# A gated delta-rule layer on one core: the older step's po and pu directly behind the newer step's px, fewer transfers, a reordered substitution

## The chip, the core and the metric

The kernel runs on one of the eight cores of a Trainium2 chip. A core has five engines with a queue of instructions each, worked through in order: TensorE (PE; its weight loads are shown apart as PEld), VectorE (DVE), ScalarE (ACT), GpSimd (POOL) and SyncE (SP), which here issues every DMA. Engines wait for one another through semaphores. [...] The metric is the device time of one execution in microseconds; less is better. Everything is float32.

## The reference

Input x is 4 sequences of 1024 rows of 256. Two residual blocks follow each other: x + layernorm(attention(layernorm(x))), and the same with a small gated feed-forward network. The attention is a gated delta rule in chunks of 64 rows, with 16 key heads, 32 value heads and 128 numbers in each head. Cut to what matters:

```python
mixed = silu(causal_conv4(x @ W_qkv.T));  q, k, v = split(mixed)      # q, k are normalized
A  = -((k * beta) @ k.T * decay) * strictly_lower
Tm = inverse(I - A)                                                    # 64 x 64, unit lower triangular
u, kcd = Tm @ (v * beta), Tm @ (k * beta * exp(gc))
def step(S, chunk):                                                    # 16 chunks, in order
    attn  = (q @ k.T) * decay
    v_new = u - kcd @ S
    out   = (q * exp(g)) @ S + attn @ v_new
    S     = S * exp(g_last) + (k * exp(g_last - g)).T @ v_new
```

The outputs are normalized by their mean square, multiplied by silu of a second projection z of x, and projected to 256 columns. The feed-forward network looks its weights up in a table of 16 numbers.

## The kernel before, in words

**Tiling.** Four value heads with their two key heads make a group; there are eight groups. A tile is a chunk of 64 rows of two sequences (halves `ab` of 128 partitions); the four sequences are two pairs, and steps alternate between the pairs, each with its own state S. A `Super` is eight steps (four chunks of both pairs) of one group, so there are 32 supers and 256 steps. The time goes into one loop of 277 slots, in which five stages of different supers lie on top of each other, so that every slot holds work for every engine.

**The generators.** Each kind of work is a Python generator that is resumed piece by piece:
- `channel` (L407): one projection of 128 columns into `pp`, the convolution on ACT (`cv`, L454) and three DVE instructions (L457), and silu (L461). Slot letter B for q and k, A for v.
- `norms` (n), `scores` (s): norms of q and k; `kkq`, the products of the chunk with itself, times the decay `dc`, into `lT` and `aT`, which go to DRAM as `ltd` and `atd`.
- `invert` (v1, v2): reads blocks of 16 from `ltd` as `lb` (L610) and inverts them by 15 pairs of DVE instructions (`rank`, `v`; L627, L629), one pair to each v1 but for the first, which calls the load. The loads of `xh` (L620) stand in its second part.
- `join` (c): puts two 16-blocks together to one of 32. ACT copies `vh_s` go to DRAM (`vth`, `vh`) and come back as the zero-padded operands `padh1` and `padh2`; products `mh1` (L662) and `mh2` (L678); the result `ndh` goes through DRAM back into `v`.
- `build` (b): the same from 32 to 64 with `pad1`, `pad2`, `mt`, `m1` (L731) and `m2` (L745). The inverse lies in DRAM as `ued`.
- `expand` (L760): loads a step's inverse `ue`, its scores `ae` (two DMAs), and `qku` (q and k).
- `step`: N0 transposes v (`pv`, L786); N1 multiplies the state (`pkqs`, L799), DVE makes `x0` (L810), ACT `qs`; N2 makes `px` (L819 transposes of k, L823 with the inverse), ACT takes `xs` and `kt` from it. In the slot after it the same generator goes on as the older one: O3 makes `po` (L848), DVE adds `core` (L862); J squares `core` on ACT; O4 makes `pu` (L875), and DVE updates S in eight instructions (L891).
- `project_out`: Z is `pz` (L145, called from L923) and its silu, POOL multiplies twice (L927, L929); T transposes (`pto`, L933) and U projects (`pout`, L940); DVE adds into `ac` (L945), which is loaded from and stored to `acc_d` for every step (L919, L949).

**What sets the order.** `SLOTS` (L1003) is the order written out by hand, one string for each of eight slots; the instructions of PE, ACT, DVE and POOL keep the order in which they are called, apart from the pieces after a `yield` of a number, which `go` resumes that many places later. SP's DMAs are placed by the framework's own scheduler. PSUM has a ring of four banks (`bank`) and one of two double banks (`two_banks`, for pp and pu): a product waits until the reader of the fourth (second) one before it is done. After the loop comes the feed-forward network, whose first part runs in the last 16 slots.

Of the kernel before, what the change touches and what calls it, by code (L numbers as in the profile page):

```python
# [14 lines left out]
P = 128  # L15
# [50 lines left out]
def delta_net_ffn_kernel(  # L66
# [258 lines left out]
    with ExitStack() as main:  # L325
# [19 lines left out]
        padh1 = w1.tile([P, NQ, C], F32, tag="padh1", name="padh1")  # L345
        padh2 = w1.tile([P, NQ, P], F32, tag="padh2", name="padh2")
        mh = w1.tile([P, NQ + 1, HB], F32, tag="mh", name="mh")
        for t in (*pads, xh, padh1, padh2, mh):
            G_.memset(t, 0.0)
        ueds = [dram.tile([P, SB * HG, C], F32, name=f"ued{i}") for i in range(3)]  # L350
        for t in ueds:
            nc.sync.dma_start(t.rearrange("p w i -> p (w i)"), pads[0].rearrange("p w i -> p (w i)"))
        states = [w1.tile([P, MG, 2, 2, P], F32, tag=f"S{p}", name="S") for p in range(NPAIR)]
# [190 lines left out]
        def scores(k, blk):  # L544
# [22 lines left out]
            for n, (u0, dc) in enumerate(zip(us, dcs)):  # L567
# [15 lines left out]
                stores = []  # L583
                for name, j, dst in (("lT", 0, k.ltd), ("aT", 1, k.atd)):
# [7 lines left out]
                    stores.append((dst[:, u0 : u0 + 2, :, :], o))  # L592
                yield 2
                for to, o in stores:
                    nc.sync.dma_start(to, o)

# [7 lines left out]
        def invert(k):  # L604
# [9 lines left out]
            yield  # L614
            for s in range(2):
                us = slice(s * SB // 2, (s + 1) * SB // 2)
                for q in range(4):
                    rows = slice(s * C + q * HB, s * C + (q + 1) * HB)
                    src = k.ltd[q * BS : q * BS + HB, us, :, q % 2 * BS + HB : (q % 2 + 1) * BS]
                    nc.sync.dma_start(xh[rows, :, s * HB : (s + 1) * HB], src.rearrange("j u h i -> j (u h) i"))  # L620
            l2, v2 = halves(lb), halves(v)
            for j in range(HB - 1):
# [5 lines left out]
                to = v2[:, :, 0 : j + 1, j + 1 :]  # L628
                V.tensor_tensor(to, to, t, ALU.subtract)  # L629
                if j < HB - 2:  # L630
                    yield
            k.lb, k.v = square(lb), square(v)

        def join(k):
# [16 lines left out]
            for s in range(2):  # L651
                for z in range(4):
                    rows = slice(z * BS + s * HB, z * BS + (s + 1) * HB)
                    u = s * 4 + z
# [20 lines left out]
            for h in range(HG):  # L675
                for q in range(4):
                    g = q * HG + h
                    T_.matmul(  # L678
                        ps[q * BS : (q + 1) * BS, h * P : (h + 1) * P],
                        lhsT=mh[:, g : g + 2, :].rearrange("p g c -> p (g c)"),  # L680
                        rhs=padh2[:, g, :],
                        start=True,
                        stop=True,
                    )
            nb = sc.tile([P, 2 * NQ, HB], F32, tag="mt", name="nbh")
            A.activation(
                nb.rearrange("p (u h) i -> p h u i", h=HG),
                ps.rearrange("p (h u i) -> p h u i", h=HG, i=HB),
                AF.Copy,
                scale=-1.0,  # L690
            )
            nc.sync.dma_start(k.ndh, nb)
# [5 lines left out]
        def build(k):  # L698
# [6 lines left out]
            for q in range(4):  # L705
                hb = slice(q % 2 * BS, (q % 2 + 1) * BS)
                to = k.ued[q * BS : (q + 1) * BS, :, hb]
                nc.sync.dma_start(to.rearrange("c w i -> w c i"), k.v[q * BS : (q + 1) * BS])
# [13 lines left out]
            for ab in range(2):  # L722
                gs = slice(ab * NQ // 2, (ab + 1) * NQ // 2)
                for z in range(4):
                    q = slice(z * BS, (z + 1) * BS)
                    nc.sync.dma_start(pad2[q, gs, q], k.ued[ab * C + BS : (ab + 1) * C, z::4, BS:])
            yield
# [26 lines left out]
            for ab in range(2):  # L754
                for hb in range(2):
                    q = slice((2 * ab + hb) * BS, (2 * ab + hb + 1) * BS)
                    to = k.ued[ab * C : ab * C + BS, hb * NQ : (hb + 1) * NQ, BS:]
                    nc.sync.dma_start(to, nb[q])

        def expand(k, u):  # L760
# [12 lines left out]
        def step(k, u):  # L773
# [18 lines left out]
            if not first:  # L792
                got = []
                for j in range(2):
# [11 lines left out]
                    got.append(ps)  # L806
                qs = t4("qs")
                for h in range(HG):
# [11 lines left out]
            for n in range(2):  # L820
                for m in range(MG):
                    for ab in range(2):
# [6 lines left out]
                        )  # L829
            xs = sc.tile([P, 2, 2, P], F32, tag="xs", name="xs")  # L830
            for ab in range(2):
                A.activation(xs[:, ab], pxs[ab][:, : 2 * P].rearrange("p (h d) -> p h d", h=2), AF.Copy, scale=-1.0)
            if not last:
                kt = sc.tile([P, 2, 2, P], F32, tag="kt", name="kt")
                for ab in range(2):
                    for n in range(2):
# [27 lines left out]
            yield  # L864
            junk = sc.tile([P, P], F32, tag="junk", name="junk")
            for h in range(HG):
                A.activation(junk, core[:, h, :], AF.Square, accum_out=k.ms[:, u, h : h + 1])  # L867
            yield
            if not last:
# [17 lines left out]
                else:  # L887
                    flat = S_.rearrange("p m a h d -> p (m a h) d")
                    made = pu.rearrange("p a (n d) -> p (a n) d", d=P)
                    for i in range(2 * HG):  # L890
                        V.scalar_tensor_tensor(  # L891
                            flat[:, i, :], flat[:, i, :], el[:, ti, i : i + 1], made[:, i, :], ALU.mult, ALU.add
                        )

        def rms(k, blk):
# [16 lines left out]
        def project_out(k, u):  # L912
# [35 lines left out]
            yield 2  # L948
            nc.sync.dma_start(acc_d[ti], ac)  # L949

# [36 lines left out]
        def work(kind, n, *args):  # L987
# [15 lines left out]
        SLOTS = [  # L1003
# [8 lines left out]
        ]  # L1012
# [154 lines left out]
        with tc.manual_schedule(engines=COMPUTE):  # L1167
            for s in range(-LQ, len(units)):
# [13 lines left out]
                if nq < len(supers):  # L1182
                    gens["B"] = channel(supers[nq], iq // 4, iq % 4, 1)
                inv = work(invert, nq - 1 if iq >= 4 else nq - 1)
                made = work(build, nq - 2)
# [118 lines left out]
```

## Time and profile before

| | |
|---|---|
| median of 3 runs | 4227.92 us (4226.19 to 4230.51) |
| the profiled execution, its own time | 4217.89 us |
| its span | 4216.2 us |
| busy: PE, DVE, ACT, POOL | 3950.7, 2919.3, 2806.3, 1930.9 us |
| first pv to last pv (the loop's steps) | 255.9 to 3889.8 us |
| DMA | 1.45 million packets, 539 MB, 52% of 16 engines |
| PE waits for DVE core before pz | 51.8 us, 32 times |
| DVE waits for lb before the first rank | 237.3 us, 32 times |

A line of the order of time gives start, duration, engine, source line, operation, output<-inputs, shape and count; in brackets stands the idle time before it and what ended it. A shape such as 64*128 is rows times columns of the array that a matmul uses. The chain of work that ended last is followed back from the end, at each step to what released it. Matmul ends are modelled, starts are measured, so the time of a group of matmuls is best taken from its start to the next group's.

### The profile page before, as it was taken

Reading aid. Unit: us, or ns where it says so; the run is one execution under the profiler, and the core shown is the slowest. Engines: PE = TensorE matmul, PEld = TensorE weight load, DVE = VectorE, ACT = ScalarE, POOL = GpSimd, SP = SyncE. Lnnn points to the kernel's source line nnn. Section 1 sums busy time; section 2 is a strip of 40 time slices with the busy share of each in tenths; the row PEclk is TensorE's granted clock in tenths of the full one; section 3 lists DMA queues with packets and bytes.
Section 4 is the critical chain, followed back from the end, with each engine's and each line's share of the span. In section 5 each row is a group of like instructions: output and inputs, shape, how many; then the busy total and the mean of one; then the engine's idle time right before and its main releaser. Section 6 shows DMA issues by size and latency. Waiting matters only on the chain.

```text
span 4216.2 us, 97070 instructions
## 1 busy us (share of the span) xinstructions
PE 3950.7 (94%) x34688; PEld 2672.5 (63%) x34688; DVE 2919.3 (69%) x7123; ACT 2806.3 (67%) x7477; POOL 1930.9 (46%) x1685
## 2 busy tenths in 40 slices
PE   3679999999999999999999999999999999999999
PEld 2456666666666666666667666666666666666454
DVE  4577777777777777777667877777777777766143
ACT  2467777777777777777777777777777777765111
POOL 2644554555455545554454545455453334334122
PEclk7789999999999999999999999999999999999999
DMA  3555555555555555655565556555655555553011
GB/s 97 156 125 130 124 133 138 135 140 134 135 146 141 134 135 141 151 142 133 135 149 140 129 137 148 140 136 141 149 136 143 130 138 141 144 123 96 24 46 24
DMA packets 1449918, 539.46 MB, mean 128 GB/s; under 512 B 1130960, under 2 KB 1393248, under 8 KB 1449056
## 3 DMA queue, kind: packets, MB, share of 16 engines
q1 hardware_dynamic: 1449440, 533.25, 52.0%
q8 instruction: 280, 4.59, 0.5%
q14 instruction: 198, 1.62, 0.1%
HBM read 292.82 MB, written 239.62 MB: 126 GB/s over the span
## 4 chain that ended last, share of the span: by engine, by line
PE 70%; DVE 8%; SPq 7%; ACT 6%; DMA 5%; issue 2%; POOL 1%; DVEq 0%; POOLq 0%; ACTq 0%
PE pp L440 16%; PE pout L940 10%; PE pz L145 8%; PE pkqs L799 8%; PE pu L875 5%; DVE cv L457 5%; PE pgu L1104 4%; PE pto L933 3%; PE px L823 3%; PE po L848 3%; PE pv L786 3%; SPq L610 2%; PE kkq L575 2%; PE py L1120 2%; DMA lb<-ltd 2%
## 5 line engine op out<-in xcount | busy, mean ns | idle before, releaser
L457 DVE SCALAR_TENSOR_TENSOR cv<-pp,cw,cv 128x512 f32<-128x512 f32 x1536 | 1150.4, 749 | 380.6 <-ACT cv L454 344.8
L927 POOL TENSOR_TENSOR zs<-zs,rr 128x512 f32<-128x512 f32 x256 | 266.2, 1040 | 909.2 <-ACT zs L925 909.0
L454 ACT ACTIVATE cv<-pp,cw 128x512 f32<-128x512 f32 x512 | 352.8, 689 | 333.3 <-PE pp L440 331.7
L440 PE MATMUL pp<-xnT,wq 128*128 128x262 f32 x2048 | 510.0, 391 | 45.0 <-DVE cv L457 26.6
L145 PE MATMUL pz<-wzs,xnT 128*64 128x512 f32 x2048 | 493.8, 603 | 51.8 <-DVE core L862 51.8
L940 PE MATMUL pout<-wo,oT 128*128 128x256 f32 x2048 | 514.5, 394 | 14.9 <-ACT oT L935 7.5
L440 PE MATMUL pp<-xnT,wv 128*128 128x262 f32 x2048 | 510.5, 390 | 15.2 <-DMA wv<-in_wqkv 13.9
L891 DVE SCALAR_TENSOR_TENSOR S<-S,dkm,pu 128x128 f32<-128x128 f32 x1792 | 480.8, 341 | 0.0
L799 PE MATMUL pkqs<-S,qku 128*64 128x256 f32 x3840 | 468.5, 386 | 0.9 <-DMA qku<-qkd 0.9
L440 PEld LDWEIGHTS pp<-xnT,wq 128*128 128x128 f32 x2048 | 374.0, 193 | 107.0 <-issue 42.6
L940 PEld LDWEIGHTS pout<-wo,oT 128*128 128x128 f32 x2048 | 370.8, 191 | 103.6 <-ACT cv L454 25.8
L440 PEld LDWEIGHTS pp<-xnT,wv 128*128 128x128 f32 x2048 | 377.2, 190 | 93.4 <-issue 24.0
L862 DVE TENSOR_TENSOR core<-po,qs 128x256 f32<-128x256 f32 x480 | 180.6, 418 | 293.8 <-PE po L848 263.5
L867 ACT ACTIVATE junk<-core 128x128 f32<-128x128 f32 x1024 | 316.1, 309 | 44.8 <-DVE core L862 19.6
L799 PEld LDWEIGHTS pkqs<-S,qku 128*64 128x64 f32 x3840 | 253.8, 136 | 136.0 <-ACT x L790 3.0
L627 DVE TENSOR_TENSOR rank<-v,lb 128x30 f32<-128x30 f32 (+7 forms) x480 | 172.1, 359 | 237.8 <-DMA lb<-ltd 237.3
L929 POOL TENSOR_TENSOR zs<-zs,core 128x512 f32<-128x512 f32 x256 | 327.5, 1279 | 20.1
L559 POOL TENSOR_TENSOR dc<-dc,dkm 128x512 f32<-128x512 f32 x128 | 133.8, 1046 | 392.9 <-DMA dc<-rows_d 256.3
L908 POOL TENSOR_TENSOR rr<-rr,rsqrt 128x16 f32<-128x16 f32 x64 | 186.9, 2921 | 265.2 <-DVE rr L900 265.2
L461 ACT ACTIVATE vt<-cv 128x512 f32<-128x512 f32 x256 | 161.4, 630 | 220.4 <-DVE cv L457 212.7
L145 PEld LDWEIGHTS pz<-wzs,xnT 128*64 128x64 f32 x2048 | 143.7, 138 | 248.4 <-issue 150.8
L317 POOL TENSOR_SCALAR lt<-lx,lutb 128x344 f32<-128x344 int32 (+2 forms) x210 | 278.5, 1326 | 16.7
(190 smaller groups left out, 7039.4 us busy)
## 6 DMA issues: line engine op xcount, KB each, us to landing
qkd<-qk SPq DMA_DIRECT2D x256, 256.0 KB
qku<-qkd SPq DMA_DIRECT2D x256, 256.0 KB
dc<-rows_d SPq DMA_DIRECT2D x128, 256.0 KB
ltd<-lT SPq DMA_DIRECT2D x128, 256.0 KB
atd<-aT SPq DMA_DIRECT2D x128, 256.0 KB
ae<-atd SPq DMA_DIRECT2D x512, 64.0 KB
ue<-ued SPq DMA_DIRECT2D x256, 128.0 KB
acc_d<-ac SPq DMA_DIRECT2D x256, 128.0 KB
```

Of the source, the lines that this page charges most:

```text
L145: T_.matmul(ps[ab * C : (ab + 1) * C, :], lhsT=xnT[:, kc, 2 * p + ab, H + n * C : H + (n + 1) * C], rhs=rhs(kc), start=kc == 0, stop=kc == ...
L317: G_.tensor_scalar(o[:n, :cols], ix[:n, :cols], float(e), lutb[:n, e : e + 1], ALU.is_equal, ALU.mult)
L440: T_.matmul(ps[:, 2 * p : 2 * p + 2, : H + BT], lhsT=wt[:, kc, :], rhs=xnT[:, kc, 2 * p : 2 * p + 2, c0 : c0 + H + BT], start=kc == 0, sto ...
L454: A.activation(cv, ps[:, :, H : H + BT], AF.Copy, scale=cw[:, ch, H : H + 1])
L457: V.scalar_tensor_tensor(cv, ps[:, :, i : i + BT], cw[:, ch, i : i + 1], cv, ALU.mult, ALU.add)
L799: T_.matmul(as4(ps)[ab * C : (ab + 1) * C, two, :], lhsT=qk[:, j, ab, m, :], rhs=S_[:, m, ab], start=True, stop=True,)
L867: A.activation(junk, core[:, h, :], AF.Square, accum_out=k.ms[:, u, h : h + 1])
L875: T_.matmul(as4(pu[:, m])[:, 2 * ab + n, :], lhsT=kt[half, ab, n, :], rhs=xs[half, ab, n, :], start=True, stop=True,)
L891: V.scalar_tensor_tensor(flat[:, i, :], flat[:, i, :], el[:, ti, i : i + 1], made[:, i, :], ALU.mult, ALU.add)
L927: G_.tensor_tensor(zs, zs, bc(k.rr[u // 4][:, u % 4, :].unsqueeze(2), h4), ALU.mult)
L929: G_.tensor_tensor(zs, zs, k.cores.pop(u), ALU.mult)
L940: T_.matmul(pp[:, :HID], lhsT=oT[:, h, :], rhs=wo[:, h, :], start=h == 0, stop=h == HG - 1)
```

## The change

1. `SLOTS` is written anew. In every slot O3 and O4 (po and pu of the older step) stand directly behind N2 (px of the newer one), before U; before, O3 stood ahead of N0 and O4 ahead of N1. J follows U. In slots 0 to 2 the join's and build's products move in the same way behind O4, and `build` gets a fifth part. The v1 of slot 3, which calls the load of `lb`, stands behind N0 instead of first; the v1s of slot 4 stand behind U, those of slots 5 to 7 partly behind U.
2. In `step`, the squares come last; `xs` and `kt` are made half by half; `qs`, `xs` and `kt` have two buffers.
3. `atd` is laid out by step, key head, row and column, so that `expand` needs one DMA for `ae` and the store of `aT` takes two. `ued` is laid out by row, half, head and column; pad2 is loaded with four DMAs instead of eight.
4. `padh2` is gone: the join uses `pads[0]`, whose diagonal blocks of 16 it fills. At the end of `build` four POOL memsets clear the blocks that the join needs empty.
5. The `xh` loads are called with the fifth rank pair instead of ahead of the first.
6. `ac` holds two steps: one load and one store for two.

```diff
-        padh2 = w1.tile([P, NQ, P], F32, tag="padh2", name="padh2")
...
-                k.atd = sd.tile([P, SB, HG, C], F32, tag="atd", name="atd")
+                k.atd = sd.tile([SB, MG, C, 2 * 2 * C], F32, tag="atd", name="atd")
...
-            for s in range(2):
-                us = slice(s * SB // 2, (s + 1) * SB // 2)
-                for q in range(4):
...
-                    nc.sync.dma_start(xh[rows, :, s * HB : (s + 1) * HB], src.rearrange("j u h i -> j (u h) i"))
...
+                if j == 4:
+                    for s in range(2):
...
+                            nc.sync.dma_start(xh[rows, :, s * HB : (s + 1) * HB], src.rearrange("j u h i -> j (u h) i"))
...
-                        padh2[rows, :, u * HB : (u + 1) * HB], k.vh[u].rearrange("q h i c -> i (q h) c")
+                        pads[0][rows, :, rows], k.vh[s * 4 + z].rearrange("q h i c -> i (q h) c")
...
+            yield
+            if k is not supers[-1]:
+                for q in range(4):
+                    rows = slice(q * BS, (q + 1) * BS)
+                    G_.memset(pad1[rows, :, q * BS : q * BS + HB], 0.0)
...
-            nc.sync.dma_start(ue, k.ued[:, u * HG : (u + 1) * HG, :])
-            for m in range(MG):
-                src = k.atd[:, u, 2 * m : 2 * m + 2, :].rearrange("(a j) h i -> j a h i", a=2)
-                nc.sync.dma_start(ae[m * C : (m + 1) * C], src)
+            nc.sync.dma_start(ue, k.ued[:, :, u * HG : (u + 1) * HG, :].rearrange("j a h i -> a j (h i)"))
+            nc.sync.dma_start(ae.rearrange("p a h i -> p (a h i)"), k.atd[u].rearrange("m j x -> (m j) x"))
...
-            ac = sc.tile([P, HID], F32, tag="ac", name="ac", bufs=3)
-            if k.g:
-                nc.sync.dma_start(ac, acc_d[ti])
+            two = acc_d[ti - u % 2 : ti - u % 2 + 2].rearrange("t p d -> p t d")
+            if u % 2 == 0:
+                k.ac = sc.tile([P, 2, HID], F32, tag="ac", name="ac", bufs=2)
+                if k.g:
+                    nc.sync.dma_start(k.ac, two)
...
-            "c A O3 s N0 n J O4 N1 Z T B n N2 U n s c",
-            "A O3 N0 J O4 N1 r Z s T B N2 q U c",
-            "c A O3 N0 J O4 N1 b Z s T B N2 n U b",
-            "v1 A O3 N0 J O4 N1 Z T B N2 U s b",
-            "A v1 b O3 s N0 v1 n J O4 N1 Z v1 T B n N2 v1 U n s",
-            "A v1 O3 N0 v1 J O4 N1 r Z s v1 T B N2 q v1 U",
-            "A v1 O3 N0 v1 J O4 N1 Z s v1 T B N2 n v1 U",
-            "A v1 O3 N0 v1 J O4 N1 Z v1 T B N2 c U s",
+            "c A s N0 n N1 Z n T B N2 O3 O4 c U J n s",
+            "A N0 N1 Z s T B N2 O3 O4 c U J r q",
+            "c A N0 N1 b Z s T B N2 n O3 O4 U J b",
+            "A N0 v1 N1 Z T B N2 O3 O4 b U J s",
+            "A s N0 n N1 Z b n T B N2 O3 O4 U v1 J n v1 s v1",
+            "A N0 v1 N1 Z s v1 T B N2 O3 O4 U v1 J r q v1 b",
+            "A N0 v1 N1 Z s T v1 B N2 n O3 O4 U v1 J v1",
+            "A N0 v1 N1 Z v1 T B N2 O3 O4 U v1 J v1 c s",
```

More of the change, by code (lines that the diff above doesn't have):

```diff
@@ L345, in delta_net_ffn_kernel @@
         padh1 = w1.tile([P, NQ, C], F32, tag="padh1", name="padh1")
-        padh2 = w1.tile([P, NQ, P], F32, tag="padh2", name="padh2")
         mh = w1.tile([P, NQ + 1, HB], F32, tag="mh", name="mh")
-        for t in (*pads, xh, padh1, padh2, mh):
+        for t in (*pads, xh, padh1, mh):
             G_.memset(t, 0.0)
-        ueds = [dram.tile([P, SB * HG, C], F32, name=f"ued{i}") for i in range(3)]
+        ueds = [dram.tile([C, 2, SB * HG, C], F32, name=f"ued{i}") for i in range(3)]
         for t in ueds:
-            nc.sync.dma_start(t.rearrange("p w i -> p (w i)"), pads[0].rearrange("p w i -> p (w i)"))
+            nc.sync.dma_start(t.rearrange("j a w i -> (j a) (w i)"), pads[0].rearrange("p w i -> p (w i)"))
         states = [w1.tile([P, MG, 2, 2, P], F32, tag=f"S{p}", name="S") for p in range(NPAIR)]
@@ L583, in scores @@
                 stores = []
-                for name, j, dst in (("lT", 0, k.ltd), ("aT", 1, k.atd)):
+                for name, j in (("lT", 0), ("aT", 1)):
                     o = sc.tile(sh, F32, tag=name, name=name)
@@ L591, in scores @@
                     )
-                    stores.append((dst[:, u0 : u0 + 2, :, :], o))
+                    stores.append(o)
                 yield 2
-                for to, o in stores:
-                    nc.sync.dma_start(to, o)
+                nc.sync.dma_start(k.ltd[:, u0 : u0 + 2, :, :], stores[0])
+                for ab in range(2):
+                    x = slice(ab * 2 * C, (ab + 1) * 2 * C)
+                    nc.sync.dma_start(
+                        k.atd[u0 : u0 + 2, :, :, x].rearrange("u m j x -> j (u m) x"),
+                        stores[1][ab * C : (ab + 1) * C].rearrange("p u (m h) i -> p (u m) (h i)", m=MG),
+                    )
         def square(t):
@@ L614, in invert @@
             yield
-            for s in range(2):
-                us = slice(s * SB // 2, (s + 1) * SB // 2)
-                for q in range(4):
-                    rows = slice(s * C + q * HB, s * C + (q + 1) * HB)
-                    src = k.ltd[q * BS : q * BS + HB, us, :, q % 2 * BS + HB : (q % 2 + 1) * BS]
-                    nc.sync.dma_start(xh[rows, :, s * HB : (s + 1) * HB], src.rearrange("j u h i -> j (u h) i"))
             l2, v2 = halves(lb), halves(v)
@@ L629, in invert @@
                 V.tensor_tensor(to, to, t, ALU.subtract)
+                if j == 4:
+                    for s in range(2):
+                        us = slice(s * SB // 2, (s + 1) * SB // 2)
+                        for q in range(4):
+                            rows = slice(s * C + q * HB, s * C + (q + 1) * HB)
+                            src = k.ltd[q * BS : q * BS + HB, us, :, q % 2 * BS + HB : (q % 2 + 1) * BS]
+                            nc.sync.dma_start(xh[rows, :, s * HB : (s + 1) * HB], src.rearrange("j u h i -> j (u h) i"))
                 if j < HB - 2:
@@ L653, in join @@
                     rows = slice(z * BS + s * HB, z * BS + (s + 1) * HB)
-                    u = s * 4 + z
                     nc.sync.dma_start(
-                        padh2[rows, :, u * HB : (u + 1) * HB], k.vh[u].rearrange("q h i c -> i (q h) c")
+                        pads[0][rows, :, rows], k.vh[s * 4 + z].rearrange("q h i c -> i (q h) c")
                     )
@@ L680, in join @@
                         lhsT=mh[:, g : g + 2, :].rearrange("p g c -> p (g c)"),
-                        rhs=padh2[:, g, :],
+                        rhs=pads[0][:, g, :],
                         start=True,
@@ L685, in join @@
             nb = sc.tile([P, 2 * NQ, HB], F32, tag="mt", name="nbh")
[L686 to L691, printed above, removed]
+            for s in range(2):
+                A.activation(
+                    nb.rearrange("p (s u h) i -> p s h u i", s=2, h=HG)[:, s],
+                    ps.rearrange("p (h u s i) -> p s h u i", h=HG, s=2, i=HB)[:, s],
+                    AF.Copy,
+                    scale=-1.0,
+                )
             nc.sync.dma_start(k.ndh, nb)
@@ L706, in build @@
                 hb = slice(q % 2 * BS, (q % 2 + 1) * BS)
-                to = k.ued[q * BS : (q + 1) * BS, :, hb]
+                to = k.ued[hb, q // 2, :, hb]
                 nc.sync.dma_start(to.rearrange("c w i -> w c i"), k.v[q * BS : (q + 1) * BS])
@@ L721, in build @@
                     nc.sync.dma_start(pad1[q, :, q], k.vtd[at : at + NQ].rearrange("w c j -> c w j"))
[L722 to L726, printed above, removed]
+            for z in range(4):
+                q = slice(z * BS, (z + 1) * BS)
+                src = k.ued[BS:, :, :, BS:].rearrange("c a (u h) i -> c (a u) h i", h=HG)
+                nc.sync.dma_start(pad2[q, :, q], src[:, :, z, :])
             yield
@@ L756, in build @@
                     q = slice((2 * ab + hb) * BS, (2 * ab + hb + 1) * BS)
-                    to = k.ued[ab * C : ab * C + BS, hb * NQ : (hb + 1) * NQ, BS:]
+                    to = k.ued[:BS, ab, hb * NQ : (hb + 1) * NQ, BS:]
                     nc.sync.dma_start(to, nb[q])
+            yield
+            if k is not supers[-1]:
+                for q in range(4):
+                    rows = slice(q * BS, (q + 1) * BS)
+                    G_.memset(pad1[rows, :, q * BS : q * BS + HB], 0.0)
         def expand(k, u):
@@ L806, in step @@
                     got.append(ps)
-                qs = t4("qs")
+                qs = t4("qs", 2)
                 for h in range(HG):
@@ L829, in step @@
                         )
-            xs = sc.tile([P, 2, 2, P], F32, tag="xs", name="xs")
+            xs = sc.tile([P, 2, 2, P], F32, tag="xs", name="xs", bufs=2)
+            kt = sc.tile([P, 2, 2, P], F32, tag="kt", name="kt", bufs=2)
             for ab in range(2):
                 A.activation(xs[:, ab], pxs[ab][:, : 2 * P].rearrange("p (h d) -> p h d", h=2), AF.Copy, scale=-1.0)
-            if not last:
-                kt = sc.tile([P, 2, 2, P], F32, tag="kt", name="kt")
-                for ab in range(2):
+                if not last:
                     for n in range(2):
@@ L864, in step @@
             yield
[L865 to L868, printed above, removed]
             if not last:
@@ L893, in step @@
                         )
+            yield
+            junk = sc.tile([P, P], F32, tag="junk", name="junk")
+            for h in range(HG):
+                A.activation(junk, core[:, h, :], AF.Square, accum_out=k.ms[:, u, h : h + 1])
         def rms(k, blk):
@@ L916, in project_out @@
             ti = k.t0 + u
-            ac = sc.tile([P, HID], F32, tag="ac", name="ac", bufs=3)
-            if k.g:
-                nc.sync.dma_start(ac, acc_d[ti])
+            two = acc_d[ti - u % 2 : ti - u % 2 + 2].rearrange("t p d -> p t d")
[3 more added lines that the diff above has]
+                    nc.sync.dma_start(k.ac, two)
+            both, ac = k.ac, k.ac[:, u % 2, :]
             pz = bank("pz")
@@ L948, in project_out @@
             yield 2
-            nc.sync.dma_start(acc_d[ti], ac)
+            if u % 2:
+                nc.sync.dma_start(two, both)
         def drain(*gens):
@@ L1183, in delta_net_ffn_kernel @@
                     gens["B"] = channel(supers[nq], iq // 4, iq % 4, 1)
-                inv = work(invert, nq - 1 if iq >= 4 else nq - 1)
+                inv = work(invert, nq - 1)
                 made = work(build, nq - 2)
```

## The prediction

> **What bounds the kernel now.** I read the shares of the engines first, then the chain that ended last, then the waits, then the instructions of one step in order of time.
>
> ```profile
> PE 3950.7 (94%) x34688; PEld 2672.5 (63%) x34688; DVE 2919.3 (69%) x7123; ACT 2806.3 (67%) x7477; POOL 1930.9 (46%) x1685
> PE 70%; DVE 8%; SPq 7%; ACT 6%; DMA 5%; issue 2%; POOL 1%; DVEq 0%; POOLq 0%; ACTq 0%
> DVE rank L627 <- DMA lb<-ltd: 237.3, 32, 11.7
> PE pz L145 <- DVE core L862: 51.8, 32, 3.3
> ```
>
> PE is the bound; the granted clock is 1.00 from 320 to 3472 us, so nothing is to be had from it. The rest of the chain has a pattern: once in each of the 32 groups of eight steps DVE waits about 7.4 us for lb, the substitution's input, everything queued behind stands, and PE then waits for core.
>
> One step with no wait in it, from the order of time on PE (start, duration as modelled; I use only differences of starts):
>
> ```profile
> 1836.05 1.93 PE L440 MATMUL pp<-xnT,wv 128*128 128x262 f32 x8
> 1837.91 0.67 PE L848 MATMUL po<-xs,ae 64*64 64x128 f32 x16
> 1838.51 0.66 PE L786 MATMUL pv<-ident,vt 128*128 128x128 f32 x4
> 1839.09 1.16 PE L875 MATMUL pu<-xs,kt 64*128 64x128 f32 x16
> 1840.18 1.95 PE L799 MATMUL pkqs<-S,qku 128*64 128x256 f32 x16
> 1841.96 1.89 PE L145 MATMUL pz<-wzs,xnT 128*64 128x512 f32 x8
> 1843.78 0.66 PE L933 MATMUL pto<-ident,zs 128*128 128x128 f32 x4
> 1844.27 1.93 PE L440 MATMUL pp<-xnT,wq 128*128 128x262 f32 x8
> 1846.04 0.38 PE L819 MATMUL px<-ident,qku 128*128 128x128 f32 x2
> 1846.35 0.67 PE L823 MATMUL px<-x,ue 64*64 64x128 f32 x16
> 1846.95 1.99 PE L940 MATMUL pout<-wo,oT 128*128 128x256 f32 x8
> ```
>
> The reader is to see that a change of array shape costs. The same eight pp matmuls take 1.77 us where another 128*128 group follows (1844.27 to 1846.04) and 1.86 where po at 64*64 follows. Within px the quartets start 109 ns apart, but 160 after the first and 220 from the last quartet to pout. pkqs to pz, both 128*64, shows neither. So leaving a shape costs 0.09 to 0.11 us (I take 0.095), and entering one 0.05 (px, po, pkqs, kkq, 64 columns), 0.056 (four transposes), 0.10 (pout, pp, pu: 320 ns against 216 for pout's first), 0.024 (the 32-column groups).
>
> Over 2886 us (200 steps) in the middle, each PE group against the lower quartile of its own kind and neighbours leaves 105 us of waits, 4.2 us per eight steps of 115.8. By place in the eight: 2.6 in the one step behind lb, 0.66 in the next (px and pto, late from the same), about 0.85 at changes of weights (wv, wo).
>
> **The change part by part.**
>
> *PE's order.* Counted from both programs' instruction order between the first projection and the last po, shape changes fall from 2136 to 1451. In an ordinary step pp-po-pv-pu-pkqs and px-pout (seven changes) becomes px-po-pu-pout and pp-pv-pkqs (five); the join's and build's 32-column groups and pn now stand beside groups that change shape anyway. Leaving: 685 x 0.095 = 65 us. Entering, by kind: before 512 x 0.051 + 505 x 0.056 + 365 x 0.104 + 240 x 0.102 + 264 x 0.05 + 192 x 0.024, with px's transposes 3, is 138 us; after 97. Sum 105 us off PE, which is the path. Two prices are not in the trace: px to po without a change, and po to pu (64*64 to 64*128). Nearest rows: pkqs to pz (free) and pv to pu (0.20). I take these. If px to po cost as a change (256 x 0.15), the saving is 67; if po to pu were free (240 x 0.2), 153.
>
> [...]
>
> *lb earlier against its use.* The first rank moves from the second place of slot 4 to behind U there; lb's call stays near the start of slot 3. Before, lb was issued at 2194.97 to 2198.15, landed 4.4 us after it was issued last, and its reader had waited 8.2 us. Its issue stands behind the same stores and pads as before; the reader comes some ten PE groups later (about 11 us) and one step's work is more even, so it lands with well over 5 us to spare. 2.6 + 0.66 us per eight steps go: 3.3 x 31 = 102 us. What is late next is the other end of the substitution:
>
> *The join.* The last two rank pairs now run behind S and ac of slot 7 instead of before them, and mh1 stands behind pu in slot 0. Rows of before:
>
> ```profile
> 2135.61 0.69 ACT L637 COPY vh_s<-v 128x256 f32<-128x256 f32 x1
> 2136.74 2.83 SPq L642 DMA_DIRECT2D vh<-vh_s  x4
> 2140.16 4.06 SPq L648 DMA_DIRECT2D padh<-vth  x8
> 2150.19 0.65 PE L662 MATMUL mh<-padh,xh 128*32 128x64 f32 x32
> ```
>
> vh_s to the last padh issued is 8.6 us; in the second group, where PE was early, mh followed 1.66 us after that, so the way is 10.3 us; PE came after 14.6. New: from the end of po in slot 7, core and S end at 4.8, ac 5.2, two rank pairs (0.46 and 0.44) 6.2, mh1 may start at 16.5 to 17.3. PE's own way there: pu 1.1, pout 1.95, pp 1.77, pv 0.53, pkqs 1.8, pz 1.9, pn 1.0, pto 0.55, pp 1.77, px 0.8, po 0.6, pu 1.15 = 15 us. A new wait of 1.4 to 2.2; I take 1.7 (bounds 0, if ranks are early, and 2.5) x 31 = 53 us. Behind mh1 on PE are pout, pn, the next pp.
>
> *S against pkqs.* S has to be done between pu and the next step's pkqs, with only pout, pp, pv between. From px's transposes at T (1846.04): ACT cv starts +0.20, three DVE cv end +3.16, core 0.75, S 2.14: +6.05. PE: 0.31 + 0.5 + 0.6 + 1.09 + 1.83 + 1.77 + 0.53 = T + 6.63, and the last part of S is read about 0.5 later. One microsecond to spare. It is used up where ACT is late: slots with vh_s and with the 2.0 us lb copy, where also oT comes about 0.35 late for po's bank. I take 0.7 us per eight steps (0 to 2.5): 22 us. pz's wait for core has gone with it, since its bank is now freed by ac.
>
> *The build.* m1 goes behind pu of slot 3, m2 behind pz of slot 4; four ued<-nb stores and ue follow on SP before the next slot's px. nb 0.6, stores 4 x 0.50, ue 0.53 and two landings of at most lb's 4.4 us are 12 us; PE's groups between m2 and that px come to 17 (pn, pto, pp, px, po, pu, pout, pn, pp, pv, pkqs, pz, kkq, pto, pp). Nothing is counted; if it failed, the excess over 17 would be paid once in eight steps. Norms and scores keep their slots, with dc, ltd and cd issued a few PE groups to either side.
>
> *Transfers.* SP issues about 500 fewer (ae 512 to 256, pad<-ued 256 to 128, ac and acc_d halved, atd 128 more). At 0.598, 0.607, 0.585/0.383 and 0.326 us each that is about 300 us of SP's time, none of it on the path where SP does not end a wait; beyond lb I count nothing. Cover: PE's step of 14 us; without it the px waits of 0.4 per eight steps would be its size. xh's eight loads move behind lb or stay early, each long before mh1.
>
> *POOL.* Four memsets per build more. Nearest rows: 128x32 at 157 ns, 128x1056 at 978, so 0.6 to 1.2 us per eight steps, 37 us at most in all, on an engine 46% busy, between two zs products that wait for ACT (909 us idle). I count nothing; the bound is 37.
> [...]
>
> *Smaller.* Squares (J) behind pu, kt interleaved with xs, qs, xs and kt twofold: ACT's work is the same, beside PE. In the last 20 steps, where pout waited for oT, po and pu now lie in between: 6 us off. The lead-in to 320 us, bound by latencies, plus or minus 15.
>
> Sum: -105 - 102 + 53 + 22 - 6 = -138 us against the profiled execution's 4217.9 (span 4216.2): 4080. The median of the runs is 10 us above that execution: **4090**.
>
> **The rivals.**
>
> *A, as summed*, 4045 to 4140.
>
> *B, no new wait.* DVE's light steps let the ranks end early, mh1 is not late, S never: 53 + 22 more, and a cheap po to pu some 10 to 20: about 4005. For: ACT and DVE are idle a quarter of the time. Against: the order on DVE is fixed, ranks behind S.
>
> *C, half is given back.* mh1 at 2.5 us (78), S and oT at 2.5 us (78), px to po paid: 138 falls to about 40 to 60: 4140 to 4200.
>
> *D, slower: DVE sets the step through S.* Place: pkqs waiting for S. If DVE is late by L us in every step, PE loses L - 1.0; the gain of all else is 105 + 102 + 6 - 53 = 160 us, 0.64 in each of 250 steps, so it decides from L = 1.64. At L = 2.0 it is 0.36 x 250 = 90 us slower, 4318. For: rank slots hold up to 15.3 us of DVE work in a 15.0 us step. Against: the four others hold 9 to 11, and DVE is 74% busy (344 of 463 us).
>
> *E, the moved order does nothing*, since the shape change is hidden elsewhere and lb's wait turns up at mh1: within 0.2%, 4228.
>
> **How the numbers follow.** A 57%, B 17%, C 13%, E 3%, D 10%. Faster or slower by over 0.2% (8.5 us, about what a measurement can tell): faster A+B+C = 0.87, same 0.03, slower 0.10. The range reaches over B and C and leaves out D, E and B's last third: 4005 to 4200.
>
> **What would show it.** Right: pp to pv 1.77, pv to pkqs 0.53, px to po 0.50 us; no rank wait for lb; pz without waits for core; mh's first matmul late by 1.4 to 2.2 us. Wrong: pkqs waiting for DVE S in most steps, px to po at 0.6, or SP as the releaser of px or po.

## The result, and the profile after

The changed kernel takes 4394.31 us (median of 4 runs, 4391.85 to 4404.35) against 4229.22 us for the kernel before: the ratio is 1.0397, 95% interval 1.0383 to 1.0411. It is 4% slower where 3% faster was forecast, and it lies outside the forecast range of 4005 to 4200. The profiled execution of the changed kernel took 4391.85 us, its span is 4390.1.

The page of the kernel after, shares of the engines and the chain that ended last:

```profile
PE 3978.4 (91%) x34688; PEld 2788.2 (64%) x34688; DVE 2921.3 (67%) x7123; ACT 2768.6 (63%) x7509; POOL 1965.2 (45%) x1808
...
PE 49%; DVE 15%; DMA 11%; ACT 9%; SPq 6%; issue 4%; POOL 1%; ACTq 0%; DVEq 0%; POOLq 0%
```

PE has the same instructions, but its part of the chain fell from 70% to 49%; DVE, DMA and ACT took the rest. Now one step with no wait in it, in order of time on PE (start, duration, engine, line, operation):

```profile
1984.68 0.60 PE L793 MATMUL pv<-ident,vt 128*128 128x128 f32 x4
1985.21 1.95 PE L806 MATMUL pkqs<-S,qku 128*64 128x256 f32 x16
...
1991.38 0.67 PE L830 MATMUL px<-x,ue 64*64 64x128 f32 x16
1991.87 0.62 PE L854 MATMUL po<-xs,ae 64*64 64x128 f32 x16
1992.41 1.16 PE L877 MATMUL pu<-xs,kt 64*128 64x128 f32 x16
1993.51 1.99 PE L949 MATMUL pout<-wo,oT 128*128 128x256 f32 x8
1995.34 1.93 PE L439 MATMUL pp<-xnT,wv 128*128 128x262 f32 x8
1997.11 0.38 PE L793 MATMUL pv<-ident,vt 128*128 128x128 f32 x2
```

From pv to pv it is 12.43 us; the same slot (slot 7) took 12.73 before. The starts are those forecast: px to po 0.49, pv to pkqs 0.53, pp to pv 1.77. So the step without waits did become shorter. The waits ate it (columns of the view: engine and line, what was waited for, us in total, times, longest):

```profile
PE pkqs L806 <- DMA qku<-qkd: 55.8, 22, 4.5
PE po L854 <- ACT zs L934: 51.4, 27, 4.7
PE po L854 <- ACT oT L944: 35.4, 91, 1.6
...
ACT lb L708 <- DMA v<-ndh: 116.2, 31, 7.5
ACT vh_s L642 <- DVE v L627: 87.8, 32, 3.6
...
SPq L762 <- ACT nb L757: 160.4, 32, 9.5
```

The DVE wait for lb (237.3 us before) and PE's wait for core (51.8) are gone, as forecast. But every line above is new or has grown. In the kernel before, SP's wait for nb was 1.5 us, the next was small, and the others were not there:

```profile
ACT lb L703 <- DMA v<-ndh: 17.4, 21, 1.5
```

Where this falls shows in the time from each slot's pv to the next, a mean over the same 25 groups of eight in the middle of each trace (slots by their place in `SLOTS`; e9, e6 and e14 are experiments below):

| slot | before | after | e9 | e6 | e14 |
|---|---|---|---|---|---|
| 0 | 15.66 | 18.56 | 15.49 | 15.32 | 15.42 |
| 1 | 14.82 | 15.02 | 14.81 | 14.53 | 14.54 |
| 2 | 13.66 | 17.11 | 13.61 | 14.79 | 13.73 |
| 3 and 4 | 32.35 | 27.96 | 29.34 | 28.94 | 28.78 |
| 5 | 13.47 | 17.17 | 13.31 | 13.81 | 13.59 |
| 6 | 13.12 | 12.82 | 13.12 | 12.82 | 12.82 |
| 7 | 12.73 | 12.42 | 12.73 | 12.42 | 12.42 |
| eight steps | 115.8 | 121.1 | 112.4 | 112.6 | 111.3 |

Slots 3 and 4 stand together, because m2 moved from one to the other. 5.25 us more per eight steps, 31 times, is 163 us, which is the whole result. If every step gained the 0.30 us of slots 6 and 7, the shape changes gave 2.4 us per eight steps, slots 3 and 4 gave another 3.8, and slots 0, 2 and 5 took 3.2, 3.75 and 4.0 (slot 1: 0.5).

Slot 2 in one group, SP, ACT and PE, in order of time:

```profile
2269.36 0.56 SPq L463 DMA_DIRECT2D qkd<-qk  x1
...
2270.02 2.79 SPq L697 DMA_DIRECT2D ndh<-nbh  x1
...
2272.86 1.93 SPq L634 DMA_DIRECT2D xh<-ltd  x3
...
2276.60 1.90 SPq L701 DMA_DIRECT2D v<-ndh  x4
...
2280.04 1.93 ACT L708 COPY lb<-v 128x1024 f32<-128x1024 f32 x1 [5.52 <-DMA v<-ndh]
2281.87 0.59 ACT L934 ACTIVATE zs<-pz 128x512 f32<-128x512 f32 x1
...
2282.51 0.69 PE L854 MATMUL po<-xs,ae 64*64 64x128 f32 x4 [3.43 <-ACT zs L934]
```

The build's copy of `lb` on ACT waits 5.5 us for the join's result to come back from DRAM; zs stands behind it on ACT, and po needs the PSUM bank that zs reads. Slot 5 in one group:

```profile
1461.87 1.06 SPq L762 DMA_DIRECT2D ued<-nb  x2
...
1464.54 0.57 SPq L777 DMA_DIRECT2D qku<-qkd  x1
...
1467.85 0.60 PE L793 MATMUL pv<-ident,vt 128*128 128x128 f32 x4
...
1470.95 2.59 PE L806 MATMUL pkqs<-S,qku 128*64 128x256 f32 x16 [2.51 <-DMA qku<-qkd]
```

`expand` of a group's first step, which also loads `qku`, is called at the name O4 of slot 4. With O4 at the slot's end, qku is issued behind the stores ued<-nb. PE is ready for pkqs 3.9 us after that issue began (1468.44), but qku has landed only 6.4 us after it, and pkqs waits 2.5 us.

### The profile page after: what moved, and what is told of

Same layout as the page of the kernel before. It is cut to its first block, busy times and chain, and to the rows that moved or that the text cites. A ratio compares the mean times of both kernels' runs of the same rounds, so it can differ in the third digit from the quotient of the medians.

```text
span 4390.1 us, 96477 instructions
## 1 busy us (share of the span) xinstructions
PE 3978.4 (91%) x34688; PEld 2788.2 (64%) x34688; DVE 2921.3 (67%) x7123; ACT 2768.6 (63%) x7509; POOL 1965.2 (45%) x1808
## 4 chain that ended last, share of the span: by engine, by line
PE 49%; DVE 15%; DMA 11%; ACT 9%; SPq 6%; issue 4%; POOL 1%; ACTq 0%; DVEq 0%; POOLq 0%
PE pp L439 8%; PE pkqs L806 7%; PE pout L949 7%; PE pz L145 6%; DVE cv L456 4%; PE pgu L1114 4%; PE pu L877 3%; DMA ndh<-nbh 3%; DMA qku<-qkd 3%; DVE v L627 3%; DVE S L893 3%; PE pto L942 2%; DVE rank L625 2%; PE po L854 2%; PE py L1130 2%
## 5 line engine op out<-in xcount | busy, mean ns | idle before, releaser
L806 PE MATMUL pkqs<-S,qku 128*64 128x256 f32 x3840 | 496.9, 403 | 69.3 <-DMA qku<-qkd 55.8
L949 PE MATMUL pout<-wo,oT 128*128 128x256 f32 x2048 | 532.0, 404 | 7.8 <-ACT kt L843 4.2
L949 PEld LDWEIGHTS pout<-wo,oT 128*128 128x128 f32 x2048 | 382.7, 197 | 94.2 <-issue 18.1
L818 ACT ACTIVATE qs<-pkqs,dkm 128x128 f32<-128x128 f32 x960 | 274.7, 372 | 224.6 <-PE pkqs L806 224.5
L806 PEld LDWEIGHTS pkqs<-S,qku 128*64 128x64 f32 x3840 | 273.2, 142 | 220.0 <-issue 111.9
L843 ACT ACTIVATE kt<-px,cd 128x128 f32<-128x128 f32 x960 | 309.2, 390 | 0.0
L934 ACT ACTIVATE zs<-pz 128x512 f32<-128x512 f32 x256 | 152.8, 597 | 246.6 <-PE pto L942 227.5
L460 ACT ACTIVATE qk<-cv 128x512 f32<-128x512 f32 x256 | 163.3, 638 | 210.7 <-DVE cv L456 210.6
L877 PE MATMUL pu<-xs,kt 64*128 64x128 f32 x3840 | 291.3, 293 | 0.0
L854 PE MATMUL po<-xs,ae 64*64 64x128 f32 x4096 | 209.1, 282 | 90.3 <-ACT zs L934 51.4
```

Of the source, the lines that this page charges most:

```text
L806: T_.matmul(as4(ps)[ab * C : (ab + 1) * C, two, :], lhsT=qk[:, j, ab, m, :], rhs=S_[:, m, ab], start=True, stop=True,)
L843: A.activation(kt[:, ab, n, :], pxs[ab][:, 2 * P : 3 * P], AF.Copy, scale=k.cd[:, ab, blk, un, n : n + 1],)
L854: T_.matmul(pos[m][ab * C : (ab + 1) * C, n * P : (n + 1) * P], lhsT=ae[m * C : (m + 1) * C, ab, n, :], rhs=xs[m * C : (m + 1) * C, ab, n, :],
L877: T_.matmul(as4(pu[:, m])[:, 2 * ab + n, :], lhsT=kt[half, ab, n, :], rhs=xs[half, ab, n, :], start=True, stop=True,)
L949: T_.matmul(pp[:, :HID], lhsT=oT[:, h, :], rhs=wo[:, h, :], start=h == 0, stop=h == HG - 1)
```

## The experiments

Each run is compared with the kernel before on the same chip (4220 to 4223 us there, on four chips). Beside the changed kernel it took 4229, so a difference to the changed kernel in us holds to within 7 us; the ratios have no such offset. "Stall" means the time by which PE's groups exceed the lower quartile of their own kind and neighbours, summed over 25 groups of eight; times 32/25 it is the loop's. A constant loss is not in it.

### Slot 5: qku's load

```diff
-            qku = sc.tile(...)            # in expand, with its load
+        def operands(k, u):               # qku alone
...
+                if ahead:
+                    operands(*ahead)      # at the start of the slot before the step
```

> The changed kernel, but qku of a super's first step is called at the start of the slot like every other step's, not with ue and ae after O4. Theory: in slot 5 pkqs stands because qku is queued on SP behind the four ued<-nb stores, which wait for ACT nb (160 us, 5.0 each). Of slot 5's 114 us of PE waits in 25 supers the pkqs part (53 + 20 + 8) goes: 81/25 x 32 = 100 us, 4290 us; all of it 4250. Rival (pkqs waits because DVE's S or the DMA engines are late): no change, 4394.

Measured: 4285.13 us, ratio 1.0154 [1.0133, 1.0175], 109 us below the changed kernel (103 by the ratios). Slot 5 fell from 17.17 to 14.03 and the wait for qku is gone; slots 0 and 2 stand within 0.3 us of what they were. The late call was a loss of its own, and the largest that one edit took back.

### Slot 2: the lb copy alone moved

```diff
-            "c A N0 N1 b Z s T B N2 n O3 O4 U J b",
+            "c A N0 N1 Z s T B N2 n O3 O4 b U J b",
```

> The changed kernel, but the build's first part (the lb copy on ACT and the stores behind it) in slot 2 stands behind O4 instead of behind N1. Theory: ACT stands at this copy until v<-ndh has landed, and zs, oT, cv and so po's PSUM bank wait behind it: 95 us of PE waits in 25 supers go, 122 us in all, 4272 us. Rival (ACT simply has too much work in slot 2, the copy's 2 us above all): the wait moves with it, over 4350 us.

Measured: 4361.25, ratio 1.0324 [1.03, 1.0349], 33 us below the changed kernel (31 by the ratios) instead of 122. Slot 2's stall went from 95 us to none (13.30 us flat), but m1 in slot 3 now waited for pad<-ued and pad<-vtd (28.0 and 26.5 us) and slot 4's pkqs for qku: 44 and 25 us of stall in these slots. The copy's place is what stops PE in slot 2, and the chain behind it, ued and vtd to DRAM and back into the pads, has no time to give.

### The parts alone

`e5` keeps the new layouts, the missing padh2 and the paired ac; step, SLOTS and the xh loads are those of the kernel before, with one more b at slot 5's end. `e4` is e5 with the new step and O3 O4 behind N2 in every slot, first expand called at N0:

```diff
-            "A O3 N0 J O4 N1 r Z s T B N2 q U c",
+            "A N0 N1 Z s T B N2 O3 O4 U J r q c",
```

> The kernel before with the new layouts and transfers alone (atd, ued, pad2, ac by twos, padh2 replaced by pads[0] with the four memsets); order of the slots, of the step and of the xh loads as before. Theory: transfers are beside PE's work; between 4205 and 4235 us. Rival (the transfers or memsets carry the loss): over 4300 us.

> As the run with the transfers alone, and O3, O4 behind N2 and J behind U (with the second buffers of qs, xs, kt, and r, q behind J); the places of c, b, n, s, v1 and the call of the first step's loads as before. Theory: 0.31 us less in each of 250 steps, 78 us below the run with the transfers alone, some of it lost to S and oT: 4140 to 4180 us. Rival (D of the prediction: pkqs waits for S in every step): above the run with the transfers alone.

Measured: e5 4182.03, ratio 0.9907 [0.9884, 0.993]; e4 4217.47, ratio 0.9988 [0.9976, 1.0]. Both expectations missed. The transfers were not free of effect: they gained 40 us. The order alone, on top of them, lost 35 us, though its slots 6 and 7 took 12.82 and 12.42 us as forecast. Its stall lies in slot 2 (88 us of it): the lb copy waits 108.7 us for v<-ndh, 64.4 in e5. The time is the rival's, but its reason is not there: pkqs never waited for S.

### The chain called earlier

In the kernel before, the older step's po, junk and pu stood ahead of the lb copy in slot 2. Without them ACT comes to the copy sooner. So mh2 was called earlier:

```diff
-            "A N0 N1 Z s T B N2 O3 O4 U J r q c",
-            "c A N0 N1 b Z s T B N2 O3 O4 n U J b",
+            "A N0 N1 Z s T c B N2 O3 O4 U J r q c",
+            "A N0 N1 b Z s T B N2 O3 O4 n U J b",
```

That is e6, on e4. e7 is the same move on e1, e9 on e5. e8 is e7 with the ranks at the places of the kernel before ("v1 A N0 ..." in slot 3, "A v1 N0 v1 ..." in slots 5 to 7).

> The step order alone (the kernel of the run e4) with the join's second product, mh2, issued in the middle of slot 1 (between pto and the qk channel) instead of at its end, and the loads v<-ndh called at slot 1's end. Theory P (place against chain): from mh2 to the lb copy there is a chain of transfers of about 9 us that does not shrink, and the change lets ScalarE reach the lb copy some 1.5 to 3 us earlier, because the older step's po, junk and pu no longer stand ahead of it in the slot. Five us more for the chain then end the wait: ACT lb <- DMA v<-ndh falls from 108.7 us to under 20, slot 2 from 16.8 to about 13.3 us, the time from 4217 to 4090-4130. Theory Q (SyncE's queue: the loads and stores behind ScalarE's junk hold ndh and v<-ndh wherever they are called): the lb wait stays over 70 us and the time over 4180.

> The changed kernel with both: the load of qku at the start of the slot before its step (run e1) and mh2 in the middle of slot 1. Theory P: against e1's 4285 the slot-2 wait goes (88 us in 25 groups of eight, 112 in 32): 4170-4200; what is left over the sum predicted is the wait for mh1 and vh_s behind VectorE's last rank, some 40 us in 25 groups, plus 16 of pu in slot 1 and 35 in slot 5. Theory Q: over 4240. If the build's chain behind lb is itself too long (as in the run with the late lb copy), the wait shows up in slot 3 as m1 waiting for pad<-ued and the gain is under half.

> e7 and the ranks of the inversion called where the kernel before calls them (the first at slot 3's start, the last in slot 7 before the silu stage of Z), so that VectorE ends the last rank earlier. Theory: vh_s no longer waits for the last rank (87.8 us in the changed kernel, none before), mh1 is not late, slot 0 loses its 40 us in 25 groups: another 40 to 55 us off e7, 4120-4155. Rival: the ranks are then in the way of VectorE's x0 or cv chains, and what slot 0 gains is paid in slots 4 to 7 (their undisturbed 15.0, 13.2, 13.4, 14.5 us grow): within 15 us of e7.

> The transfers alone (run e5, old step order) with mh2 in the middle of slot 1. Theory P: the lb wait of e5 (64 us) and the m1 wait behind it (22 us in 25 groups) go: 4182 - 57*1.28 = 4110, at most 4140. Theory Q: 4170 or more. Against e6 this gives what the step order is worth once the chain is fed early: by the 0.30 us per undisturbed step that all runs show, e6 should be 30 to 75 us below e9; if e6 is not below e9, the order brings waits that eat all of its gain.

Measured: e6 4127.33, ratio 0.9768 [0.9749, 0.9788]; e7 4199.5, 0.9947 [0.9932, 0.9962]; e8 4182.38, 0.9899 [0.9884, 0.9914]; e9 4126.3, 0.977 [0.9756, 0.9785]. Theory P's times held for e6 and e9 and e7; its wait in e6 did not:

```profile
ACT lb L707 <- DMA v<-ndh: 64.0, 31, 5.0
```

In e6 the four v<-ndh took 5.3 us to issue behind qkd. So theory Q has its part, and means over all groups of eight show how large it is (us after slot 2's first pv; the last row is the start of the copy less its mean wait for v, that is, when ACT came to it):

| | before | e5 | e4 | after | e6 | e10 | e14 |
|---|---|---|---|---|---|---|---|
| mh2 ends on PE | -2.5 | -2.5 | -1.9 | -3.7 | -7.9 | -11.7 | -7.8 |
| last v<-ndh issued | 3.5 | 5.1 | 5.1 | 5.4 | 4.1 | -1.9 | 2.0 |
| lb copy starts | 5.4 | 6.9 | 6.8 | 7.1 | 5.8 | 3.5 | 4.5 |
| ACT came to it | 4.9 | 4.9 | 3.4 | 3.5 | 3.8 | 3.5 | 3.7 |

With the old step order (before, e5) ACT comes at 4.9, with the new one at 3.4 to 3.8. And SP issues the last v<-ndh 1.6 to 1.9 us later in e5, e4 and the changed kernel than before, in the last although mh2 ends earlier; xh, qkd and the landing of ndh stand in between in the lines of slot 2 above. Of the 3.1 us that the wait grew, 1.4 are the reader's place and 1.7 the later transfers.

e8 gained 17 us instead of 40 to 55, which is nearer to its rival: slot 0 became 2.6 us shorter per group, but slots 2 and 4 became 1.5 and 0.75 longer. And e6 stood level with e9: the order's undisturbed slots are 54 us shorter per 25 groups, its stall 59 us longer.

### Which call, and where

Three versions of e6 moved the calls again (e10: mh2 ahead of Z and v<-ndh ahead of O4; e11: lb copy behind Z; e12: both):

```diff
-            "A N0 N1 Z s T c B N2 O3 O4 U J r q c",
+            "A N0 N1 c Z s T B N2 O3 c O4 U J r q",      # e10, e12
-            "A N0 N1 b Z s T B N2 O3 O4 n U J b",
+            "A N0 N1 Z b s T B N2 O3 O4 n U J b",        # e11, e12
```

> The run e6 with its chain called earlier once more: mh2 ahead of Z in slot 1, v<-ndh ahead of O4 in slot 1. In e6 the v<-ndh stores ended their issue at 33.9 us after slot 0's start (the last four took 5.3 us to issue behind qkd) and the lb copy began at 35.6, where ScalarE had come to it at some 33.3: 64 us of waits. Theory: 1.5 to 3 us earlier ends most of it: the wait under 25 us, slot 2 from 14.8 to 13.3-13.8, the time from 4127 to 4080-4105. Rival (SyncE's queue sets when v<-ndh goes, not where it is called, since the issue behind qkd takes longer each): within 12 us of e6.

> The run e6 with only the lb copy moved, behind Z in slot 2, so that zs is made before ScalarE waits for v. Theory: px no longer waits for zs (28 us), the lb copy comes to its place 1 to 1.5 us later and waits 64 - 40 = 24 us; the chain behind it starts as before: 4085-4110. Rival: the wait moves on to oT and cv behind lb, as it moved on to m1 in the run with the late lb copy: within 12 us of e6.

> e10 and e11 together: slot 2 loses its whole stall (37 us in 25 groups of eight, 48 in 32): 4070-4090, the sum of undisturbed slots being 54 us per 25 groups below that of e9 (4126). If it is not below 4100, the step order's 0.27 us per step are given back elsewhere (slots 0, 5 and 6 hold 51 us in 25 groups in e6).

Measured: e10 4148.49, ratio 0.9833 [0.9819, 0.9848]; e11 4137.44, 0.98 [0.9785, 0.9814]; e12 4197.85, 0.995 [0.9935, 0.9965]. None of the three theories gave the time; for e11 its rival did. e10 did end slot 2's stall (13.30 us flat): with v there in time nothing else holds the copy. But slot 1 went to 15.17 and slot 4 to 15.45. In e11 the lb copy stood ahead of oT instead of zs, and po waited 41.6 us for oT. e12 had both losses (slot 1 15.12, slot 4 15.90, and 39.0 us of po for oT).

Two more took e10's moves apart: e14 only calls v<-ndh ahead of O4, e15 only mh2 ahead of Z.

```diff
-            "A N0 N1 Z s T c B N2 O3 O4 U J r q c",
+            "A N0 N1 Z s T c B N2 O3 c O4 U J r q",      # e14
+            "A N0 N1 c Z s T B N2 O3 O4 U J r q c",      # e15
```

> The run e6 (4127) with one move of e10's two: the stores v<-ndh called ahead of O4 in slot 1 instead of at its end, mh2 left where e6 has it. If the lb copy's place is the whole of slot 2's stall, the stores (issued from 28.6 to 33.9 us behind qkd in e6) end near 31, the wait of 64 us falls under 20 and slot 2 from 14.8 to 13.3-13.6; with slot 1 at 14.5 and slot 4 at 13.95 as in e6 the time is 4080-4100. Rival: with v early, the next group's lb load or scores come later on SyncE as in e10 (rank waits 179 us instead of 117, slot 4 15.5): 4120-4150.

> The run e6 with e10's other move: mh2 ahead of Z in slot 1, v<-ndh at the slot's end. If this move makes e10's losses (slot 1 15.17 instead of 14.53 by po->pu 0.65 us a time, slot 4 15.45 instead of 13.95), it is 4140-4165 and slots 1 and 4 stand as in e10; if they come from the early call of v<-ndh, slots 1 and 4 are as in e6 and the time is 4110-4130.

Measured: e14 4093.05 (4087.73 to 4098.84), ratio 0.9694 [0.968, 0.9709]; e15 4157.45, 0.984 [0.9822, 0.9859]. Both times are as expected (e14's wait for v is 24.4 us, where under 20 was expected; slots 1 and 4 of e15 took 15.15 and 15.66): mh2 ahead of pz is what cost slots 1 and 4. The waits of e15 that e14 lacks or has less of, e15 first, then e14:

```profile
DVE rank L631 <- DMA lb<-ltd: 180.4, 32, 8.6
PE pn L495 <- DVE x L816: 18.8, 21, 2.8
```

```profile
DVE rank L631 <- DMA lb<-ltd: 103.2, 30, 8.5
...
ACT lb L707 <- DMA v<-ndh: 24.4, 17, 3.5
```

With mh2 ahead of pz the substitution's loads come later and DVE's late ranks hold x0; by what way mh2 delays them was not tried. e14 is the version that beats both kernels: the change's step order, its layouts and its paired ac, the ranks, norms, m2 and xh at the places of the kernel before, mh2 and v<-ndh earlier than in either. PE is busy 95% of its span, and 77% of the chain that ended last is PE's.

### Which transfers

`e13` is e5 with acc_d moved step by step, as before.

```diff
-            two = acc_d[ti - u % 2 : ti - u % 2 + 2].rearrange("t p d -> p t d")
+            ac = sc.tile([P, HID], F32, tag="ac", name="ac", bufs=3)
```

> The transfers alone (run e5, 4182) with acc_d moved one step at a time as in the kernel before; the layouts of ued and atd, the fewer loads of ue, ae and pad stay. Theory R: what e5 gained came from SyncE no longer standing at every acc_d store for VectorE (159 us behind ranks in the kernel before, 5 in e5), which let the lb loads and ae go on time: without the pairs the pz wait for core (52 us, 7 in e5) is back and the time is 4205-4240. Theory S: the gain is in the fewer loads (256 ae, 128 pad less): 4175-4195.

Measured: 4205.78 (10 runs, 4190.78 to 4218.77), ratio 0.9966 [0.9953, 0.9979]. Of e5's 40 us the pairs make some 25 and the layouts some 15. Theory R's time came, its reason did not: PE's wait for core stayed gone (8.2 us), and SP stood only 27 us behind ranks at the acc_d store, 159 in the kernel before. The new layouts alone had ended that. What the pairs save is not settled; one difference on record is that SP, before it loads ac, waits for the store of acc_d 137.2 us in e13 and 41.6 in e5.

## Why the prediction was wrong, step by step

**PE's order, -105: right, in kind and about in size.** In slot 7 (medians of 25 groups) pp went from 1.86 to 1.77 us, po from 0.60 to 0.55, pv from 0.59 to 0.53 and px from 0.60 to 0.49; the other groups stayed, and the sum is the 0.31 us that the step gained. px to po and po to pu, the two prices that the trace did not have, came out close to what was taken. For the whole order, take PE's time for eight steps without its waits (the lower quartile of each group between the same neighbours): it is 111.1 us in e9 and 107.9 in e8, which has the slots of the change but for the ranks and mh2. That is 3.2 us, 101 in the loop. e14, with the products of join and build and the norms called mostly where the kernel before has them, stands at 108.7: 75 in the loop. So this term did not fail; the waits covered it.

**lb against its use, -102: right.** The rank wait is gone. Slots 3 and 4 took 4.4 us less, of which 1.2 are PE's own time; the other 3.2 are 98 us in 31 groups.

**The join, +53: the right wait, at half its size.** ACT's vh_s waited 87.8 us for DVE's last rank and mh1 came late; slot 0 took 3.2 us per group instead of 1.7, 99 us in all (3.5 us, when PE's own gain in this slot is counted at its measured 0.7 instead of 0.30). PE meets this in three places (medians): 1.1 us before pn and 1.1 inside it, since ACT's x and sq stand behind vh_s, and 1.35 before mh1. What was mis-sized is the last two rank pairs. They were taken at 0.90 us and took 2.43 on average (1.45 before), with POOL at work beside them:

```profile
2363.69 1.27 POOL L559 TENSOR_TENSOR dc<-dc,above 128x512 f32<-128x512 f32 x1
2363.74 1.30 DVE L627 TENSOR_TENSOR v<-v,rank 128x56 f32<-128x56 f32 x1
...
2365.57 0.65 ACT L642 COPY vh_s<-v 128x256 f32<-128x256 f32 x1 [2.78 <-DVE v L627]
...
2367.89 2.08 PE L495 MATMUL pn<-sq,ones 128*32 128x512 f32 x8 [1.01 <-ACT x L797]
```

In 25 groups of the kernel before, the changed kernel, e1, e7 and e8, none of these four DVE instructions took over 0.22 us without a POOL instruction beside it; with one, they took 0.94 on average in the changed kernel. In e8, where the ranks stand at their old places, none had one and the four took 0.83 us. These 1.5 us are most of what the wait came out too long. The prediction counted nothing for POOL's four memsets; these rows are of POOL's other work. With the ranks back in place slot 0 gave back 2.6 us, but most of it reappeared behind it.

**S against pkqs, +22: S never waited for.** Of pkqs's waits 55.8 us name qku. Four more, 13.3 us, name other DVE instructions, but they stand in the same slot 5, the last S had been done 0.9 us before each began, and e1 has none of them. oT for po's bank is there, 35.4 us. Rival D, which put the danger here, had the wrong mechanism and was right only that the kernel would be slower.

**The build, counted at nothing: the step that failed.** It compared the way from m2, behind pz of slot 4, to px of slot 5 (12 us against 17), and px indeed hardly waited for ue (5.3 us). (The products stand behind O4 in slots 0, 1 and 3 of the new order; slot 2 has none, against point 1 of the change.) Two things were left out. The call of a group's first `expand` hangs on the name O4, so moving O4 moved qku's load behind the stores of m2's result: 109 us (e1; 103 by the ratios). And the chain from mh2 over ndh and v to the lb copy was never worked out, because neither end seemed to move; its reader came 1.4 us earlier, past po, junk and pu, and its transfers 1.7 us later: 86 us (e7 against e1). Both are cases of a moved step whose other effects were not followed: what it was called with, and what had stood ahead of others because of it.

**Transfers, counted at nothing:** a gain of 40 us (e5), and at the same time the 1.7 us by which v comes later; with mh2 called early (e9) the gain is 96.

The forecast of 4090 was thus a time that the idea could give, but not with the calls that the change made: e14 comes within 3 us of it (10 by the ratio). That it comes so close is partly luck, since the gain of the transfers, which the sum counted at nothing, stands in it. From the changed kernel to e14: qku -109, mh2 earlier -86, ranks -17, the other calls of join, norms, m2, xh and the first expand -55, v<-ndh earlier -34.

## What to carry to other kernels

When a generator's piece is moved in a hand-written order, list all that is called at its name and all that stood behind it on every queue: here a load hung on the name, and a copy on ScalarE came 1.4 us closer to a chain of DRAM round trips that had nothing to give (the copy already waited half a microsecond for it in each group). Work out, for every chain through DRAM that crosses the moved place, its length against the distance between its two ends, even where neither end is touched. A reordering that shortens a step eats into the slack of all such chains; call their first link earlier in the same edit, and only by as much as is needed (mh2 one place further up, in e10 and e15, cost more than it gave). And when small DVE instructions move, look what POOL does at their new place (here 0.94 us each on average with POOL at work beside them, 0.22 at most without).

## What the runs showed that was not expected

**These waits cost more than their length.** The stretches around the slot 5 wait shown above (columns: window, its length, busy time and count of PE, PEld, DVE, ACT and POOL, the granted clock, DMA share, GB/s):

```profile
1467.00:1471.00 4.00, 1.49 (x11) 1.11 (x10) 3.79 (x13) 3.85 (x8) 1.87 (x2) 1.00 0.70 197
1471.00:1474.00 3.00, 3.00 (x18) 1.94 (x20) 2.93 (x10) 0.43 (x2) 0.17 (x1) 0.68 0.64 176
1474.00:1478.00 4.00, 4.00 (x30) 2.44 (x27) 1.84 (x4) 0.87 (x4) 0.00 (x0) 0.81 0.38 89
1478.00:1490.00 12.00, 11.78 (x101) 8.48 (x102) 9.38 (x29) 9.58 (x27) 6.98 (x5) 1.00 0.48 125
```

After PE had waited 2.5 us, the granted clock was 0.68 and 0.81 for the next 7 us, and from pkqs to pz it took 2.31 us instead of 1.78: by the clock some 1.7 us (3 x 0.32 + 4 x 0.19) on top of the wait. In the 25 groups the clock stood at half for 150 us, 31 times, each time 3.4 or 6.8 us, against 14 us before, 75 in e1 and none in e9. Inside these stretches the times from one matmul to the next, without a wait between them, exceed the median of the same pair outside them by 66 us, against 7 before: 60 us in 25 groups, 76 in the loop, nearly half of the slowdown. In the 25 groups of all 16 traces, such a stretch stood beside (it ran, or began within 3.5 us) 46 of the 52 PE gaps longer than 3 us, 72 of the 110 between 2 and 3 us, and 55 of the 369 between 1 and 2. Why the clock falls beside such waits is not shown. The prediction priced each new wait at its length.

**Issuing the same DMA did not take a fixed time.** The store of ndh took SP 0.34 us (median) in the kernel before and 1.99 after, with the same shape. In the changed kernel 29 of the 32 stand right behind the store of qkd, before none did. The 30 of e6's v<-ndh that stand right behind qkd took 2.5 us (median; up to 3.7), the others 0.49. qkd alone does not do it: two v<-ndh stood behind it in the kernel before and took 0.3 us. What makes the issue longer there was not tried.
